# Moving small work between engines and queues in a fused attention and expert kernel

## The chip, the cores and the metric

The kernel runs on one core of a Trainium2 chip. The core has five engines with instruction streams of their own: TensorE (PE, matrix products; its weight loads are shown apart as PEld), VectorE (DVE), ScalarE (ACT), GpSimd (POOL) and SyncE (SP), which here only issues DMA transfers. The metric is the device time of one execution in microseconds. The kernel before took 1471.6 us (median of three runs, 1470.6 to 1475.58).

## The reference

Four batches of 1024 rows with 512 features, in f32:

```python
x = x + xattn(layernorm(x), ctx, ctx)       # 16 heads of 32; query s sees the keys t < s, row 0 sees itself
x = x + ffn(layernorm(x))

# ffn, in groups of t = 32 rows
logits = einsum('bgtd,des->bgtes', grouped, controller) + tie    # 32 x 4 expert sets
perm = (logits == max over t)                                    # each expert set picks one row of a group
dispatched = einsum('bgtd,bgtes->bgesd', grouped, perm)
inner = relu(einsum('bgesd,desf->bgesf', dispatched, f1) + bias)
out = einsum('bgesd,bgtes->bgtd', einsum('bgesf,esfd->bgesd', inner, f2), perm)
```

## The kernel before, in words

**Attention** (`attention_phase`, L38 to L891). A unit `u` is one batch (`u // 4`) and one group of four heads (`u % 4`), so there are 16 units. For each, PE projects queries, keys and values (`pq` L288, `pk` L274, `pv` L307), then goes through 12 steps: two halves `h` of 512 queries, with 4 and 8 blocks of 128 keys. The scores are computed twice: with queries in the partitions (`sc`, L401 and L407) for the row maxima that VectorE takes (`nm`, L413), and transposed with the maxima subtracted (`st`, L467 and L473). ScalarE makes the exponentials `pr` from the second (L481), and GpSimd clears what the mask forbids (L484).

A step's `pr` then has two uses. PE multiplies it with the values, `av` (L517, in `weigh_values`), two steps later. And its sum over the keys, for the division of the softmax, is gathered elementwise in an accumulator: `add_sums` (L490 to L506), once for each of two groups `g` of two heads. Group 0 is added on VectorE, one step late; group 1 on GpSimd.

At the end of a half, ScalarE copies `av` to `raw` (L526), a single buffer; so the multiply that reads the earlier `raw` is finished first. `normalize` (L531) lets PE sum the accumulators (`pd`, L543), VectorE invert (`rd`, L550), and sends the inverse through DRAM to spread it over partitions: one store (L553) and four loads (L556). The multiply by it (L538) gives `atT`. The last half of all spreads the inverse with PE instead (`pb`, L577).

**Beside it.** For the next batch, `ln_rows` (L198) loads x in two halves (`xt`) and takes the row statistics on VectorE (L211, L212), then a power on GpSimd (L215) and a store of the statistics (L216). `ln_turned` (L227) loads x transposed and the statistics, spread over partitions (`both`, L235). For the batch before, `o_step` (L339) makes the output projection of a row tile (`po`, L348), adds the residual (L354), stores the sum to `x2_dram` (L355) and takes its statistics for the second layernorm (L336, L337). `load_residual` (L324) loads x of a row tile one tile ahead (L327) and adds the bias `bo_sb` on GpSimd (L328); three buffers.

**What sets the order.** A planner in the program's text does. Pieces of VectorE work are put aside with an estimated cost by `later`; `beside(0.9)` takes some from the queue at every step, and `finish(names)` does named ones at once. Matmul work waits in other queues and fills the time in which scores aren't free. PE, VectorE, ScalarE and GpSimd then execute in the order of the text (`manual_schedule`, L1123). SyncE isn't listed there: the framework places its DMAs when the program is built. Each engine executes its own stream in order, and SyncE waits in order as well.

**Routing** (L775 to L891). After the last unit the 4096 rows are taken in eight parts `q` of four row tiles. `load_tokens` loads a part of `x2_dram` (1 MB, L796); `roots` (L817) adds epsilon to variances on VectorE (L819) and raises each part to the power -0.5 on GpSimd (L822); `normalize_tokens` (L824) normalises and stores the part; `turn_tokens` transposes it on PE (`px`, L839); `choose_tokens` makes the logits (`pl`, L845) and the choice; `return_choice` transposes and stores that. The last batch's eight row tiles are projected in between by `last_row` (L800, `po` L808).

**Experts** (`ffn_phase`). The normalised rows are loaded again (`xn`, L939, eight pieces of 1 MB: a quarter of the features and half of the rows), and the choices (`perm`, L1004, in two halves); PE dispatches (`pd`, L957) and makes the first layer (`pi`, L976), then the second layer, and combines.

Of the kernel before, what the change touches and what calls it, by code (L numbers as in the profile page):

```python
# [11 lines left out]
F32 = mybir.dt.float32  # L12
# [25 lines left out]
def attention_phase(  # L38
# [159 lines left out]
    def ln_rows(b):  # L198

        stats = {}  # L200

        def load(half):
            xt = qpool.tile([P, 4, D], F32, tag="xt", name=f"xt_{b}_{half}", bufs=1)
            nc.sync.dma_start(xt, x_t[b, half])
            mv = spool.tile([P, 2, 4], F32, tag="ln_both", name=f"ln_both_{b}_{half}")
            stats[half] = (xt, mv)

        def measure(half, i):
            xt, mv = stats[half]
            st = spool.tile([P, 6], F32, tag="ln_stats", name=f"ln_stats_{b}_{half}_{i}")  # L210
            nc.vector.bn_stats(st, xt[:, i, :])  # L211
            nc.vector.bn_aggr(mv[:, :, i], st)  # L212
            if i == 3:
                nc.vector.tensor_scalar_add(mv[:, 1], mv[:, 1], EPS)
                nc.gpsimd.tensor_tensor(mv[:, 1], mv[:, 1], mhalf, ALU.pow)  # L215
                nc.sync.dma_start(  # L216
                    stats_dram[2 * b + half].rearrange("s (i p) -> p s i", p=P), mv
                )
                if half == 0:
                    load(1)  # L220

        load(0)
        for half in range(2):
            for i in range(4):
                later(("m", b, half, i), 1.0, lambda half=half, i=i: measure(half, i))

    def ln_turned(b):  # L227

        both = {}
        xnTs[b] = qpool.tile([P, NC, S], F32, tag="xnT", name=f"xnT_{b}", bufs=1)  # L230
        nc.sync.dma_start(xnTs[b], xT[b].rearrange("(c p) t -> p c t", p=P))

        def spread_stats(half):
            both[half] = qpool.tile([P, 2, HS], F32, tag="both", name=f"both_{b}_{half}", bufs=1)
            nc.sync.dma_start(both[half], stats_dram[2 * b + half].partition_broadcast(P))  # L235

        def normalize_chunk(half, c):
            xn = xnTs[b][:, c, ts(half, HS)]
            nc.vector.tensor_tensor(xn, xn, both[half][:, 0], ALU.subtract)
            nc.vector.tensor_tensor(xn, xn, both[half][:, 1], ALU.mult)  # L240
            if half == 0 and c == NC - 1:
                spread_stats(1)

        finish(*(("m", b, half, i) for half in range(2) for i in range(4)))
        spread_stats(0)
        for half in range(2):
            later(("wait", b, half), 0.9, lambda: None)
            for c in range(NC):
                later(("n", b, half, c), 1.3, lambda half=half, c=c: normalize_chunk(half, c))
# [74 lines left out]
    def load_residual(b, t):  # L324
        finish(("row", b, t - 3), ("row", b - 1, t + 5))
        xt = opool.tile([P, D], F32, tag="xr", name=f"xr_{b}_{t}", bufs=3)
        nc.sync.dma_start(xt, x[b, ts(t, P), :])  # L327
        nc.gpsimd.tensor_tensor(xt, xt, bo_sb, ALU.add)  # L328
        residuals[b, t] = xt


    moments = opool.tile([P, B * NT, 2], F32, tag="moments", name="moments")

    def measure_row(b, t, x2):
        st = opool.tile([P, 6], F32, tag="row_stats", name=f"row_stats_{b}_{t}", bufs=2)
# [3 lines left out]
    def o_step(b, t, ahead=None):  # L339

        if (b, t) not in residuals:
            load_residual(b, t)
        if ahead:
            load_residual(*ahead)
        finish(*(("at", b * NC + c, t // 4) for c in range(NC)))
        po = ps_m.tile([P, D], F32, tag="pm", name=f"po_{b}_{t}")
        for c in range(NC):
            nc.tensor.matmul(  # L348
                po, lhsT=atTs[b * NC + c][:, ts(t, P)], rhs=weights["o"][:, c, :],
                start=(c == 0), stop=(c == NC - 1),  # L350
            )
            yield (LARGE,) if c < NC - 1 else (LARGE, dve, 0.7)
        xt = residuals.pop((b, t))
        nc.vector.tensor_tensor(xt, po, xt, ALU.add)  # L354
        nc.sync.dma_start(x2_dram[ds(b * S + t * P, P), :], xt)  # L355
        later(("row", b, t), 0.9, lambda: measure_row(b, t, xt), front=True)
# [151 lines left out]
    def weigh_values(u, k):  # L508
# [12 lines left out]
        now[0] += LARGE * (HS - q0) / HS + 0.14  # L521
        if j == last:
            given(act, 0.6)
            finish(("at", u - 1 + h, 1 - h))
            raw = qpool.tile([P, HS], F32, tag="raw", name=f"raw_{u}_{h}", bufs=1)
            nc.scalar.copy(raw, avs.pop((u, h)))  # L526
            avs[u, h] = raw
        if k:
# [2 lines left out]
    def normalize(u, h):  # L531
# [18 lines left out]
        nc.vector.reciprocal(rd, pd)  # L550
        if (u, h) != (NU - 1, 1):
            n = 2 * u + h
            nc.sync.dma_start(inverse_dram[ts(n, P), :], rd)  # L553
            rows = qpool.tile([P, 4, P], F32, tag="inverse", name=f"inverse_{u}_{h}", bufs=1)
            for r in range(R):
# [136 lines left out]
    for u in range(-1, NU):  # L692
# [15 lines left out]
        if more and hc == 1:  # L708
            load_ctx(b + 1, 0)
            add("t", b + 1, [ln_step_turned(b + 1)], 0.0)  # L710
        add("v", u + 1, v_todo)
        if more and hc == 2:
            add("c", b + 1, [load_step(b + 1, 1)], 0.0)
# [7 lines left out]
        for k in range(STEPS):  # L721
# [24 lines left out]
            if u >= 0:  # L746
# [10 lines left out]
                            ensure(("o", u // NC - 1, NT - 1))  # L757
                        soon.append((now[0], normalize(u, h)))

                add_sums(u, k, 1, nc.gpsimd)  # L760
                sums.append(add_first)
                pending.append(weigh)
            slot(2 * (STEPS - k) - 1, scores_free() if u + 1 < NU else 0.0)
    while sums:
# [10 lines left out]
    ES, T = P, 32  # L775
    QN = 4
    NQ = B * S // (QN * P)
    rpool = ctx.enter_context(tc.tile_pool(name="route", bufs=2, reuse_waits="tile"))
    lpool = ctx.enter_context(tc.tile_pool(name="route_last", bufs=2, reuse_waits="tile"))
    xpool = ctx.enter_context(tc.tile_pool(name="route_x", bufs=2, reuse_waits="tile"))  # L780
    ps_o = ctx.enter_context(tc.tile_pool(name="ps_ro", bufs=2, space=PSUM, reuse_waits="tile"))
    ps_x = ctx.enter_context(tc.tile_pool(name="ps_rx", bufs=3, space=PSUM, reuse_waits="tile"))
    ps_l = ctx.enter_context(tc.tile_pool(name="ps_rl", bufs=2, space=PSUM, reuse_waits="tile"))
# [2 lines left out]
    nc.sync.dma_start(ctrl_sb, ctrl.rearrange("(c p) e -> p c e", p=P))  # L786
    tie_sb = rpool.tile([P, T], F32, tag="tie", name="tie_sb", bufs=1)
    nc.sync.dma_start(tie_sb, tie)
    rstd = opool.tile([P, B * NT], F32, tag="rstd", name="rstd")
    tokens, turned, chosen = {}, {}, {}  # L790
    LAST = NQ - NT // QN

# [7 lines left out]
    def last_row(t):  # L800
# [2 lines left out]
            tokens[q] = lpool.tile([P, QN, D], F32, tag="x2l", name=f"x2_{q}")  # L803
        if t + 1 < NT:
            load_residual(B - 1, t + 1)
        po = ps_o.tile([P, D], F32, tag="po", name=f"po_{B - 1}_{t}")
        for c in range(NC):
            nc.tensor.matmul(  # L808
# [1 line left out]
                start=(c == 0), stop=(c == NC - 1),  # L810
            )
        x2 = tokens[q][:, i, :]
        nc.vector.tensor_tensor(x2, po, residuals.pop((B - 1, t)), ALU.add)
        nc.sync.dma_start(x2_dram[ds((B - 1) * S + t * P, P), :], x2)
        measure_row(B - 1, t, x2)

    def roots(q0, q1):  # L817
        r = rstd[:, q0 * QN : q1 * QN]
        nc.vector.tensor_scalar_add(r, moments[:, q0 * QN : q1 * QN, 1], EPS)  # L819
        for q in range(q0, q1):  # L820
            rq = rstd[:, ts(q, QN)]
            nc.gpsimd.tensor_tensor(rq, rq, mhalf, ALU.pow)  # L822

    def normalize_tokens(q):  # L824
        for i in range(QN):
# [45 lines left out]
    load_tokens(0)  # L871
    load_tokens(1)
    load_residual(B - 1, 0)
    roots(0, LAST)
    normalize_tokens(0)
    for n in range(NQ + 2):
        for i in range(QN):
            if n < NQ:
# [9 lines left out]
        for t in range(2 * n, min(2 * n + 2, NT)):  # L888
            last_row(t)
        if 2 * n + 2 == NT:  # L890
            roots(LAST, NQ)  # L891


@with_exitstack
# [272 lines left out]
```

## Time and profile before

| | |
|---|---|
| median of three runs | 1471.6 us |
| profiled execution | 1467.71 us |
| its span | 1465.9 us |
| PE busy | 1393.4 us (95%) |
| VectorE busy | 927.5 us (63%) |
| ScalarE busy | 502.4 us (34%) |
| GpSimd busy | 486.6 us (33%) |
| DMA moved | 125.25 MB, mean 85 GB/s |

The profile is of one execution. Attention takes the span up to about 1144 us, routing up to about 1229, and the experts the rest. Rows of instructions give start, duration, engine, line, tile written and tiles read, and in brackets the idle time of the engine ahead of it with what ended that. Rows of stretches give each engine's busy time, then the clock that TensorE was granted (1.00 is full speed), the busy share of the DMA engines and what they moved. Rows of waits give the total, the number and the longest.

### The profile page before, as it was taken

The page shows a single profiled execution, that of the slowest core. Times are in us where ns is not written, and L with a number is a line of the kernel's source. Part 1 is how long each engine was busy: PE and PEld are TensorE (multiplying, and loading weights), DVE is VectorE, ACT ScalarE, POOL GpSimd, SP SyncE. Part 2 cuts the span into 40 slices and gives each one's busy share as a digit, 9 for nine tenths or more (in the row PEclk, how much of TensorE's full clock was granted, in tenths as well). Part 3 has the DMA queues.
Part 4 walks back from the last instruction along what each step waited for, and adds up shares of the span by engine and source line. Part 5 has one row for each costly group of instructions (what it writes and reads, how often), then busy time and mean ns, then how long its engine had stood idle before and what let it go on. Part 6 is the DMA issues. An engine that isn't in the chain of part 4 may idle for free.

```text
span 1465.9 us, 31695 instructions
## 1 busy us (share of the span) xinstructions
PE 1393.4 (95%) x13704; PEld 733.0 (50%) x13704; DVE 927.5 (63%) x1377; ACT 502.4 (34%) x785; POOL 486.6 (33%) x557
## 2 busy tenths in 40 slices
PE   6999999999899999999999999999998898997997
PEld 4344544445344533543535344434443555887887
DVE  3666777656558586666666766565674464576666
ACT  2033333323132223332322232323334123645664
POOL 1034344333425253434343434333356320000122
PEclk9999999999999999999999999999999797899999
DMA  8011202001230210011212000010112679657554
GB/s 298 26 48 35 77 24 67 20 1 41 57 105 30 89 53 10 11 56 40 86 44 62 30 19 11 10 38 10 39 39 76 222 245 327 178 164 235 184 165 146
DMA packets 96972, 125.25 MB, mean 85 GB/s; under 512 B 12992, under 2 KB 54336, under 8 KB 96704
## 3 DMA queue, kind: packets, MB, share of 16 engines
q1 hardware_dynamic: 94272, 114.84, 25.0%
q0 software_dynamic: 2560, 8.39, 1.9%
q8 instruction: 107, 1.75, 0.5%
q14 instruction: 33, 0.27, 0.1%
HBM read 91.78 MB, written 31.42 MB: 84 GB/s over the span
## 4 chain that ended last, share of the span: by engine, by line
PE 80%; issue 6%; DVE 6%; DMA 3%; POOL 2%; ACT 1%; SPq 0%; POOLq 0%; DVEq 0%; ACTq 0%
PE sc L401 12%; PE st L467 10%; PE av L517 9%; PE pq L288 8%; PE pk L274 8%; PE pv L307 8%; PE po L348 5%; PE pd L957 3%; PE sc L407 3%; DVE nm L413 2%; PE pi L976 2%; PE st L473 2%; PE po L808 2%; PE pl L845 2%; PE pd L543 2%
## 5 line engine op out<-in xcount | busy, mean ns | idle before, releaser
L413 DVE TENSOR_REDUCE nm<-sc 128x2 f32<-128x1024 f32 (+3 forms) x384 | 349.2, 951 | 264.3 <-PE sc L407 179.1
L481 ACT ACTIVATE pr<-st 128x1024 f32<-128x1024 f32 (+3 forms) x384 | 290.4, 808 | 584.3 <-PE st L473 563.1
L484 POOL TENSOR_SCALAR_AFFINE_SELECT pr<-pr 128x256 f32<-128x256 f32 x256 | 122.2, 487 | 383.5 <-ACT pr L481 381.4
L504 POOL TENSOR_TENSOR acc<-acc,pr 128x1024 f32<-128x1024 f32 (+3 forms) x128 | 209.4, 1636 | 93.3 <-ACT pr L481 85.6
L401 PE MATMUL sc<-kT,qT 32*128 32x512 f32 (+3 forms) x1536 | 206.3, 531 | 8.6 <-ACT pr L481 4.9
L467 PE MATMUL st<-qT,kT 32*128 32x512 f32 (+3 forms) x1536 | 191.1, 534 | 4.7 <-DVE nm L413 4.6
L517 PE MATMUL av<-pr,v 128*32 128x512 f32 (+3 forms) x1536 | 166.4, 501 | 7.8 <-POOL pr L484 4.3
L274 PE MATMUL pk<-ct,w_k 128*128 128x512 f32 x256 | 131.0, 629 | 9.9 <-DMA w_k<-in_wkT_dram 9.2
L307 PEld LDWEIGHTS pv<-w_v,ct 128*128 128x128 f32 x1024 | 119.5, 192 | 34.6 <-issue 24.7
L467 PEld LDWEIGHTS st<-qT,kT 32*128 32x128 f32 x1536 | 68.6, 183 | 127.6 <-issue 99.9
L401 PEld LDWEIGHTS sc<-kT,qT 32*128 32x128 f32 x1536 | 74.4, 183 | 115.4 <-issue 50.6
L504 DVE TENSOR_TENSOR acc<-acc,pr 128x1024 f32<-128x1024 f32 (+3 forms) x128 | 126.2, 986 | 9.2 <-POOL pr L484 8.9
L307 PE MATMUL pv<-w_v,ct 128*128 128x128 f32 x1024 | 131.4, 281 | 0.2 <-DMA w_v<-in_wvT_dram 0.2
L288 PE MATMUL pq<-xnT,w_q 128*128 128x512 f32 x256 | 127.3, 616 | 1.5 <-ACT xnT L194 1.5
L501 POOL TENSOR_TENSOR acc<-pr,pr 128x768 f32<-128x768 f32 (+1 forms) x32 | 66.7, 2085 | 161.5 <-ACT pr L481 161.5
L1078 POOL DMA_DIRECT2D out_dram<-xr x32 | 24.2, 757 | 238.8 <-DVE xr L1077 237.6
L348 PE MATMUL po<-w_o,atT 128*128 128x512 f32 x192 | 95.5, 616 | 0.0
L517 PEld LDWEIGHTS av<-pr,v 128*32 128x32 f32 x1536 | 32.0, 108 | 95.0 <-issue 67.2
L274 PEld LDWEIGHTS pk<-ct,w_k 128*128 128x128 f32 x256 | 43.9, 194 | 68.9 <-issue 55.0
L473 PE MATMUL st<-mxT,ones 32*128 32x512 bf16 (+3 forms) x768 | 74.6, 322 | 0.3 <-DVE mxT L444 0.3
L288 PEld LDWEIGHTS pq<-xnT,w_q 128*128 128x128 f32 x256 | 43.0, 189 | 52.9 <-issue 46.2
L967 DVE COPY disp<-pd 128x512 f32<-128x512 f32 x64 | 41.2, 686 | 33.0 <-PE pd L957 30.1
(101 smaller groups left out, 1499.7 us busy)
## 6 DMA issues: line engine op xcount, KB each, us to landing
ct<-in_ctxT_dram SPq DMA_DIRECT2D x8, 1024.0 KB, 5.1
xt<-in_x_dram SPq DMA_DIRECT2D x8, 1024.0 KB, 5.4
xr<-in_x_dram SPq DMA_DIRECT2D x32, 256.0 KB, 2.7
xn_dram<-x SPq DMA_DIRECT2D x8, 1024.0 KB, 5.7
xn<-xn_dram SPq DMA_DIRECT2D x8, 1024.0 KB, 5.5
f<-in_f_dram SPq DMA_DIRECT2D x16, 512.0 KB, 4.5
f<-in_f_dram SPq DMA_DIRECT2D x32, 256.0 KB, 5.9
xr<-x_dram SPq DMA_DIRECT2D x32, 256.0 KB, 4.7
```

The lines of the kernel that those rows point to most:

```text
L274: nc.tensor.matmul(pk, lhsT=weights["k"][:, c, ts(hc, P)], rhs=cts[b, half][:, c, :], start=(c == 0), stop=(c == NC - 1),)
L288: nc.tensor.matmul(pq, lhsT=weights["q"][:, c, ts(hc, P)], rhs=xnTs[b][:, c, ts(half, HS)], start=(c == 0), stop=(c == NC - 1),)
L307: nc.tensor.matmul(pv[:, t, :], lhsT=cts[b, half][:, c, ts(t, P)], rhs=weights["v"][:, c, ts(hc, P)], start=(c == 0), stop=(c == NC - 1),)
L348: nc.tensor.matmul(po, lhsT=atTs[b * NC + c][:, ts(t, P)], rhs=weights["o"][:, c, :], start=(c == 0), stop=(c == NC - 1),)
L401: nc.tensor.matmul(scs[r // 2][:, r % 2, :n], lhsT=qT[rr, ts(i, P)], rhs=kT[rr, ds(c0, n)], start=True, stop=not diag,)
L413: nc.vector.tensor_reduce(nm[:, c0 // HS, i % 4, ts(g, 2)], scs[g][:, :, :n], AX.X, ALU.max, negate=True)
L467: nc.tensor.matmul(scs[r // 2][:, r % 2, :n], lhsT=kT[rr, ts(j, P)], rhs=qT[rr, ds(h * HS + q0, n)], start=True, stop=False,)
L473: nc.tensor.matmul(scs[r // 2][:, r % 2, :n], lhsT=ones16[rr, :], rhs=mxT[rr, ds(q0, n)], start=False, stop=True,)
L481: nc.scalar.activation(pr[:, :, :n], scs[g][:, :, :n], AF.Exp)
L484: nc.gpsimd.affine_select(out=d, in_=d, compare_op=ALU.is_ge, fill=0.0, base=0 if j == 0 else -1, pattern=[[0, 2], [P + 1, P]], channel_mu ...
L504: engine.tensor_tensor(acc, acc, pr[:, :, :n], ALU.add)
L517: nc.tensor.matmul(avs[u, h][rr, q0:], lhsT=vs[u][:, j, rr], rhs=pr[r // 2][:, r % 2, : HS - q0], start=(j == 0), stop=(j == last),)
```

## The change

The changed kernel computes the same. It does the following.

1. `ln_rows`: two empty pieces of 0.9 go ahead of each half's statistics, and one behind; the power, the store of the statistics and the load of the second half become a piece of their own behind it. `ln_turned` finishes that piece too.
2. `load_residual` only loads; the bias is added by `residual`, called at the start of `o_step` and of `last_row`.
3. The epsilons and powers of the second layernorm: those of batches 0 and 1 are taken within attention, at the first unit of batches 2 and 3, behind the rows' statistics; at the start of routing only batch 2's remain, issued behind part 0's normalisation. Batch 3's stay where they were.
4. The `raw` of the last unit's first half takes the buffer of `both`, so the multiply isn't finished ahead of it; in `normalize` the multiply is now finished ahead of the store of the inverse.
5. In the last unit both groups of sums are added on VectorE, one step late.
6. Routing's pools are opened in another order, so its tiles lie elsewhere in SBUF.

The order of SyncE's DMAs follows from the build and changes with this. Ahead of batch 2's `both` load now stand the `inverse` loads of the unit's half before. In routing, `ctrl_sb` and `tie_sb` stand ahead of part 0's load, which waits for the last `pd`. At the dispatch, the first half of `perm` stands ahead of the first `xn` load.

```diff
@@ ln_rows
             if i == 3:
                 nc.vector.tensor_scalar_add(mv[:, 1], mv[:, 1], EPS)
-                nc.gpsimd.tensor_tensor(mv[:, 1], mv[:, 1], mhalf, ALU.pow)
-                nc.sync.dma_start(
-                    stats_dram[2 * b + half].rearrange("s (i p) -> p s i", p=P), mv
-                )
-                if half == 0:
-                    load(1)
+
+        def root(half):
+            mv = stats[half][1]
+            nc.gpsimd.tensor_tensor(mv[:, 1], mv[:, 1], mhalf, ALU.pow)
+            nc.sync.dma_start(stats_dram[2 * b + half].rearrange("s (i p) -> p s i", p=P), mv)
+            if half == 0:
+                load(1)
 
         load(0)
         for half in range(2):
+            for i in range(2):
+                later(("load", b, half, i), 0.9, lambda: None)
             for i in range(4):
                 later(("m", b, half, i), 1.0, lambda half=half, i=i: measure(half, i))
+            later(("behind", b, half), 0.9, lambda: None)
+            later(("m", b, half, 4), 0.0, lambda half=half: root(half))
@@ ln_turned
-        finish(*(("m", b, half, i) for half in range(2) for i in range(4)))
+        finish(*(("m", b, half, i) for half in range(2) for i in range(5)))
@@ load_residual
         nc.sync.dma_start(xt, x[b, ts(t, P), :])
+        residuals[b, t] = xt
+
+    def residual(b, t):
+        xt = residuals.pop((b, t))
         nc.gpsimd.tensor_tensor(xt, xt, bo_sb, ALU.add)
-        residuals[b, t] = xt
+        return xt
...
+    rstd = opool.tile([P, B * NT], F32, tag="rstd", name="rstd")
+
+    def variances(t0, t1):
+        nc.vector.tensor_scalar_add(rstd[:, t0:t1], moments[:, t0:t1, 1], EPS)
+
+    def roots(t0, t1):
+
+        for t in range(t0, t1, 4):
+            rt = rstd[:, ds(t, 4)]
+            nc.gpsimd.tensor_tensor(rt, rt, mhalf, ALU.pow)
@@ o_step
+        xt = residual(b, t)
         finish(*(("at", b * NC + c, t // 4) for c in range(NC)))
...
-        xt = residuals.pop((b, t))
@@ weigh_values
-            finish(("at", u - 1 + h, 1 - h))
-            raw = qpool.tile([P, HS], F32, tag="raw", name=f"raw_{u}_{h}", bufs=1)
+            if (u, h) == (NU - 1, 0):
+
+                raw = qpool.tile([P, 2, HS], F32, tag="both", name=f"raw_{u}_{h}", bufs=1)[:, 0]
+            else:
+                finish(("at", u - 1 + h, 1 - h))
+                raw = qpool.tile([P, HS], F32, tag="raw", name=f"raw_{u}_{h}", bufs=1)
@@ normalize
             n = 2 * u + h
+            finish(("at", u - 1 + h, 1 - h))
             nc.sync.dma_start(inverse_dram[ts(n, P), :], rd)
@@ the loop over units
+        if b > 1 and hc == 0:
+            finish(*(("row", b - 2, t) for t in range(NT)))
+            t0 = (b - 2) * NT
+            later(("variances", b), 0.3, lambda t0=t0: variances(t0, t0 + NT))
+            for half in range(2):
+                later(("behind roots", b, half), 0.9, lambda: None)
+                later(("roots", b, half), 0.0, lambda t=t0 + 4 * half: roots(t, t + 4))
...
-                add_sums(u, k, 1, nc.gpsimd)
-                sums.append(add_first)
+                if u < NU - 1:
+                    add_sums(u, k, 1, nc.gpsimd)
+                    sums.append(add_first)
+                else:
+                    sums.append(lambda u=u, k=k: (add_first(u, k), add_sums(u, k, 1, nc.vector)))
@@ routing
+    xpool = ctx.enter_context(tc.tile_pool(name="route_x", bufs=2, reuse_waits="tile"))
     rpool = ctx.enter_context(tc.tile_pool(name="route", bufs=2, reuse_waits="tile"))
     lpool = ctx.enter_context(tc.tile_pool(name="route_last", bufs=2, reuse_waits="tile"))
-    xpool = ctx.enter_context(tc.tile_pool(name="route_x", bufs=2, reuse_waits="tile"))
...
-    rstd = opool.tile([P, B * NT], F32, tag="rstd", name="rstd")
@@ last_row
+        xt = residual(B - 1, t)
...
-        nc.vector.tensor_tensor(x2, po, residuals.pop((B - 1, t)), ALU.add)
+        nc.vector.tensor_tensor(x2, po, xt, ALU.add)
...
-    def roots(q0, q1):
-        r = rstd[:, q0 * QN : q1 * QN]
-        nc.vector.tensor_scalar_add(r, moments[:, q0 * QN : q1 * QN, 1], EPS)
-        for q in range(q0, q1):
-            rq = rstd[:, ts(q, QN)]
-            nc.gpsimd.tensor_tensor(rq, rq, mhalf, ALU.pow)
...
-    roots(0, LAST)
     normalize_tokens(0)
+    variances((B - 2) * NT, (B - 1) * NT)
+    roots((B - 2) * NT, (B - 1) * NT)
...
-            roots(LAST, NQ)
+            variances((B - 1) * NT, B * NT)
+            roots((B - 1) * NT, B * NT)
```

## The prediction

> **What bounds the kernel now.** I read the page's busy shares first, then PE's waits, then the instructions around the two longest ones that the edits touch.
>
> ```profile
> PE 1393.4 (95%) x13704; PEld 733.0 (50%) x13704; DVE 927.5 (63%) x1377; ACT 502.4 (34%) x785; POOL 486.6 (33%) x557
> ...
> PE st L467 <- DVE nm L413: 4.6, 1, 4.6
> PE av L517 <- POOL pr L484: 4.3, 3, 1.8
> ...
> PE av L517 <- ACT raw L526: 3.4, 5, 2.6
> ```
>
> TensorE (PE) is busy 1393.4 of 1465.9 us and the change leaves its matmuls alone. So a gain can only come out of its 72.5 us of idle time, and out of stretches in which its clock is granted at half. The three waits (us in total, times, longest) are those that this diff can reach; together they hold 12.3 us. The largest wait of all, 9.2 us for w_k at the start, is not touched.
>
> The first wait is one event, at 375 us. SyncE's own issues, then VectorE and PE:
>
> ```profile
> 356.11 0.38 SPq L216 DMA_DIRECT2D stats_dram<-ln_both  x1
> 356.79 0.34 SPq L553 DMA_DIRECT2D inverse_dram<-rd  x1
> 367.49 0.34 SPq L235 DMA_DIRECT2D both<-stats_dram  x1
> 368.15 1.71 SPq L556 DMA_DIRECT2D inverse<-inverse_dram  x4
> ...
> 372.74 0.69 DVE L538 TENSOR_TENSOR atT<-raw,inverse 128x512 f32<-128x512 f32 x1 [7.91 <-DMA inverse<-inverse_dram]
> ...
> 375.42 1.22 PE L467 MATMUL st<-qT,kT 32*128 32x512 f32 x2 [4.62 <-DVE nm L413]
> ```
>
> The `both` load must wait until the statistics store has landed, 11.4 us after it was issued. The four `inverse` loads stand behind it in SyncE's queue, though their own store had little to wait for (elsewhere the same pair is 1.6 us apart: 1122.51 and 1124.11). The multiply into atT is 7.91 us late, the maxima behind it on VectorE are late, and PE stands.
>
> The other two waits are the last unit (`raw` 2.63, the masks on GpSimd 1.83, 1.51 and 0.96). Stretches of 15 us (PE, PEld, DVE, ACT, POOL busy; granted clock; DMA share; GB/s):
>
> ```profile
> 360.00:375.00 15.00, 10.79 (x84) 5.62 (x82) 6.37 (x9) 3.19 (x4) 4.70 (x2) 0.96 0.18 54
> 375.00:390.00 15.00, 14.59 (x63) 5.05 (x63) 7.75 (x11) 4.04 (x5) 5.68 (x6) 0.81 0.00 0
> ...
> 1110.00:1125.00 15.00, 12.37 (x100) 4.94 (x102) 6.40 (x8) 6.29 (x7) 4.82 (x3) 0.89 0.27 80
> 1125.00:1140.00 15.00, 10.71 (x116) 4.42 (x110) 4.72 (x6) 5.78 (x9) 14.32 (x14) 0.83 0.27 88
> 1140.00:1155.00 15.00, 11.15 (x46) 7.70 (x39) 6.22 (x16) 2.34 (x4) 9.05 (x9) 0.60 0.69 229
> ...
> 1230.00:1245.00 15.00, 12.34 (x160) 10.87 (x158) 6.01 (x10) 5.39 (x11) 0.00 (x0) 0.52 1.07 337
> ```
>
> At 1125 us GpSimd is busy 14.32 of 15 and sets the pace; VectorE has 10 us free.
>
> **1. SyncE's order, and the statistics' placement.** In the built order of the changed program the `inverse` loads of that unit follow their store directly, ahead of batch 2's statistics. So the 4.21 us that PE lacks at 360 to 375 come back, and of the half clock after it 15 x 0.19 = 2.85 us. The clock gate is where a rule can be set against the row. The Trainium skill ("TensorE: Matmul & The Clock Gate", Part 1) says that the clock falls to half after a window of some 3.4 us of idleness and returns after as long a busy one. The row agrees for this wait of 4.62. But by the rule the last unit's gaps (2.63, 1.83, 1.51) would cost only their own length, 6.9 us with the 0.96; the rows there show 0.89 and 0.83 as well, 15 x (0.11 + 0.17) = 4.2 us more. I go by the rows. Term A: -7.0. What may be late next: the `both` load's wait of about 11 us doesn't vanish; it now stands, near 393 to 404 us, in front of an x2 store and the next residual load. VectorE's four row statistics of the second half come in one block of 4 x (0.68 + 0.18) + 0.3 = 3.7 us. Both stand at places where PE had no wait. If that cover fails for one of the three batches, it is another event like this one, so A's range is -8 to 0.
>
> **2. Small work on GpSimd.** The residual's bias add (1.27 us each) moves from the row's load to its use; its waits for that load, 38.2 us in six, go from in front of GpSimd's masks. PE waits for GpSimd only in the last unit, so this is nothing now. Cover: VectorE needs the sum only after the row's four po matmuls, 1.85 us (half of 3.70 for eight), which is longer than 1.27; behind a big GpSimd sum (2.35) the add may come up to 2 us late for VectorE, which is 63% busy. If a residual load is late, the add still waits in GpSimd's queue with masks and sums behind it, and PE's av behind those; with the load one row ahead I see no such case. Four of the six powers (about 1.03 each) and two adds of 0.17 go into attention where GpSimd is a third busy: nothing. Sum: 0, range 0 to +2.
>
> **3. The last unit.** Eleven copies and sums move from GpSimd to VectorE. PE alone, from 1115.2 without its waits and at full clock: av, pd, st and the rest are 14.0 us of work by the rows at full clock (1.06 for an av of 512, 1.06 for a pd, 1.3 for an st), so 1129.3. VectorE from 1112 on: eight sums of 128x1024 at 1.22 = 9.8; two each of 1.14 and 0.87 and 0.60 make 5.2; xr 0.68, its statistics 0.87, rd 0.96 and two atT at 0.69: 18.9 us in all. With about 1 us of waits for exponentials it ends near 1132, and pd after it near 1133.2. Before, pd ended at 1140.74. Term L: -7.5. VectorE becomes this unit's bound. A GpSimd sum beside a VectorE one seems to slow the latter (1.43 against 1.16), so I keep 1.22. If VectorE is also late for the first exponentials, or the atT wait (landing 5.4 us after rd) holds the sums behind it, -4; if it overlaps better, -10.
>
> **4. The junction.** Before, px at 1146.63 waits 2.62 for the normalised x2_0, which had waited for the adds and the first power:
>
> ```profile
> 1140.78 0.96 DVE L550 RECIPROCAL rd<-pd 128x128 f32<-128x128 f32 x1 [2.18 <-PE pd L543]
> ...
> 1144.98 6.17 POOL L822 TENSOR_TENSOR rstd<-rstd,mhalf 128x4 f32<-128x4 f32 x6 [4.55 <-DVE rstd L819]
> ...
> 1146.63 3.68 PE L839 MATMUL px<-ident,x 128*128 128x128 f32 x16 [2.62 <-DVE x L827]
> ```
>
> That is 5.9 us after pd. The power goes from this path. But the routing pools open in another order, and the built program now gives x2_0's load (before at 1125.87, long landed) a wait for the last pd. Such a 1 MB load lands in 5.5 us (median of six), and x2_1's is right behind and shares the queues: 5.5 + 0.6 for the hand-over and a share of the second + 0.55 to normalise = about 6.7. So one wait takes the place of the other: +0.8, range -1 to +3. The clock of 0.60 at 1140 stays low, since px still waits: 0.
>
> **5. Routing to dispatch.** SyncE's order changes here too. xn_0_0 (1 MB) was read at 1207.84, while the engines still had room. It now stands behind perm h0 and a later write, at about 1225, in a stretch where DMA is at 1.02 to 1.07 of its share. The first dispatch matmuls (1229.54) need it: 1225 + 5.5 to 6.5 is 1231 to 1232. Term D: +2.5, range 0 to +7 (the upper end if all four loads queue and the half clock of 0.52 lasts longer).
>
> Sum: -7.0 + 0 - 7.5 + 0.8 + 2.5 = -11.2. The profiled execution took 1467.71 (1465.9 span and 1.8 around it): 1456.5. The median shown is 3.9 above the profiled one: 1460.4, said as 1460.
>
> **Rivals.**
> - *The wait only moves* (A = 0, perhaps +1: one such wait elsewhere). The `both` load's 11 us stand elsewhere on the same queue, and the residual loads behind them feed GpSimd. For it: the landing took as long in the other batches (11.6 at 642.60). Against: those cost PE nothing. Then 1467.
> - *VectorE fills up* (L = -3). For it: 18.9 us of work in some 20, in strict order with atT's DMA wait between. Then 1465.
> - *Slower.* One mechanism: the `both` load's 11 us wait, now ahead of the x2 stores and residual loads on SyncE in batches 1, 2 and 3, makes residuals late. GpSimd's bias add then waits with the masks behind it, PE stands for av, and the clock falls. Each such event is priced like the one at 375 us: 4.62 + 2.85 = 7.5. One gives back A; two (15.0 against 11.2) bring the time 4 above before, and three give 1467.71 - 11.2 + 22.5 = 1479.0, a median of 1483. From two events on it decides. For it: GpSimd has waited up to 10.4 us for a residual before. Against: those waits cost PE nothing, and a row's load has a whole row's time.
> - *It doesn't do what it says*: the order on SyncE changes, but the multiply at 375 and the last unit are held by something the trace hides (the exponentials, for instance): 1471.
>
> **How the numbers follow.** Forecast 0.60, own range 1453 to 1467; wait moves 0.12; VectorE fills 0.10; slower 0.10; nothing 0.08. About 0.3% (4.4 us) is what a measurement can tell from no change. Faster: 0.57 + 0.06 + 0.07 = 0.70; same: 0.03 + 0.05 + 0.02 + 0.07 = 0.17; slower: 0.01 + 0.01 + 0.10 + 0.01 = 0.13. The range from 1452 to 1474 leaves out the slower case and the best end. It takes in A and L at their small ends and D at its upper one.
>
> **What would show it.** A: no wait of st for nm above 1 us near 375, and a clock of 1.00 at 375 to 390. L: VectorE busy above 12 in the last 15 us before the last pd, the waits for masks gone, pd's end near 1133 less A's 7. Junction: px waits for a DMA of x2_0 rather than a power. D: the first pd of the dispatch with a DMA wait of 2 to 3. Wrong would be: a new PE wait for nm or masks in batches 1 to 3, or px later than 8 us after pd.

## The result and the profile after

The changed kernel takes 1482.45 us (median of 11 runs, 1474.95 to 1487.23) where the kernel before took 1473.22 beside it (11 runs). The ratio is 1.0059, with a 95% interval of 1.0036 to 1.0083: it is slower by about 9 us, where 1460 had been forecast.

The busy shares on the page of the changed kernel, and PE's waits (us in total, times, longest):

```profile
PE 1406.8 (95%) x13704; PEld 734.7 (49%) x13704; DVE 926.8 (62%) x1390; ACT 502.6 (34%) x785; POOL 474.2 (32%) x546
```

```profile
PE px L866 <- DVE x L854: 6.6, 3, 3.7
PE st L486 <- DVE nm L432: 5.8, 3, 2.7
PE pq L293 <- DVE xnT L245: 5.3, 3, 3.7
...
PE pd L986 <- DMA perm<-perm_dram: 2.6, 1, 2.6
...
PE av L536 <- POOL pr L503: 1.6, 4, 0.5
...
PE pd L986 <- DMA xn<-xn_dram: 1.3, 1, 1.3
```

The waits that the prediction aimed at have shrunk: av for GpSimd from 4.3 to 1.6, and av for `raw` is no longer among the waits. But st for nm grew from one event of 4.6 to three with 5.8, and pq now waits 5.3 us for normalised rows (`xnT`), which it didn't before. The stretches (PE, PEld, DVE, ACT, POOL busy; clock; DMA share; GB/s) show both sides:

```profile
195.00:210.00 15.00, 11.66 (x60) 4.57 (x56) 10.84 (x16) 2.33 (x5) 5.05 (x6) 0.77 0.00 0
...
360.00:375.00 15.00, 15.00 (x155) 8.22 (x153) 9.62 (x19) 5.08 (x7) 3.09 (x3) 1.00 0.02 6
375.00:390.00 15.00, 15.00 (x112) 7.62 (x110) 11.26 (x15) 5.81 (x6) 6.24 (x5) 1.00 0.08 25
...
1140.00:1155.00 15.00, 13.59 (x152) 4.67 (x144) 14.55 (x17) 8.66 (x12) 7.19 (x8) 1.00 0.27 75
```

At 360 to 390 PE is busy throughout at full clock, and in the last unit VectorE is busy 14.55 of 15 while PE goes on at 13.59. At 195 there is a new hole.

Where the time went is seen by following one instruction through both traces. The table takes the start of some row maxima (there are 384, in the same order in both), of routing's first logits add and of the last transposed copy, and gives how much later it is after than before. Both spans are of one execution.

| start in the trace before, us | later after by | added since the row above | what lies there |
|---|---|---|---|
| 103.5 | 6.5 | +6.5 | half clock twice between 62 and 83 us |
| 235.0 | 15.2 | +8.7 | batch 1's statistics: the hole at 195 (6.4 of it from 152 on) |
| 418.0 | 7.5 | -7.7 | the wait at 375 is gone |
| 614.1 | 16.2 | +8.7 | batch 2: st at 463, pq and others at 508 to 523 |
| 830.8 | 23.8 | +7.6 | batch 3: pq at 795 |
| 1093.0 | 24.6 | +0.8 | |
| 1162.5 | 16.2 | -8.4 | last unit and junction |
| 1451.0 | 18.6 | +2.4 | dispatch |

The first row isn't the change's: PE's instructions and gaps are the same there in both. The clock was half twice for 6.8 us, also in traces of kernels without part 1 (`last_only`, `before_runs` and `pools_only` below), and not in that of part 1 alone. So the two profiled executions differ by 18.7 us, but the timed runs by about 9.

### The profile page after: what moved, and what is told of

Read it like the earlier page. It is cut to its first block, busy times and chain, and to the rows that moved or that the text cites. A ratio compares the mean times of both kernels' runs of the same rounds, so it can differ in the third digit from the quotient of the medians.

```text
span 1484.6 us, 31733 instructions
## 1 busy us (share of the span) xinstructions
PE 1406.8 (95%) x13704; PEld 734.7 (49%) x13704; DVE 926.8 (62%) x1390; ACT 502.6 (34%) x785; POOL 474.2 (32%) x546
## 3 DMA queue, kind: packets, MB, share of 16 engines
q1 hardware_dynamic: 94272, 114.84, 24.6%
## 4 chain that ended last, share of the span: by engine, by line
PE 79%; DVE 7%; issue 6%; DMA 4%; POOL 2%; ACT 1%; SPq 0%; POOLq 0%; DVEq 0%; ACTq 0%
PE sc L420 12%; PE st L486 10%; PE pk L279 9%; PE pq L293 8%; PE av L536 8%; PE pv L312 7%; PE po L368 5%; DVE nm L432 3%; PE pd L986 3%; PE sc L426 3%; PE pi L1005 2%; PE st L492 2%; DMA inverse_dram<-rd 2%; PE po L842 2%; PE pl L872 2%
## 5 line engine op out<-in xcount | busy, mean ns | idle before, releaser
L503 POOL TENSOR_SCALAR_AFFINE_SELECT pr<-pr 128x256 f32<-128x256 f32 x256 | 128.2, 510 | 427.2 <-ACT pr L500 425.6
L523 POOL TENSOR_TENSOR acc<-acc,pr 128x512 f32<-128x512 f32 (+1 forms) x120 | 194.2, 1618 | 81.0 <-ACT pr L500 71.7
L420 PE MATMUL sc<-kT,qT 32*128 32x512 f32 (+3 forms) x1536 | 210.4, 537 | 8.5 <-ACT pr L500 4.1
L486 PE MATMUL st<-qT,kT 32*128 32x512 f32 (+3 forms) x1536 | 194.1, 536 | 6.1 <-DVE nm L432 5.8
L279 PE MATMUL pk<-ct,w_k 128*128 128x512 f32 x256 | 136.1, 650 | 10.1 <-DMA w_k<-in_wkT_dram 9.3
L293 PE MATMUL pq<-xnT,w_q 128*128 128x512 f32 x256 | 131.2, 631 | 6.7 <-DVE xnT L245 5.3
L523 DVE TENSOR_TENSOR acc<-acc,pr 128x1024 f32<-128x1024 f32 (+3 forms) x136 | 130.6, 967 | 0.3 <-POOL pr L503 0.3
L520 POOL TENSOR_TENSOR acc<-pr,pr 128x768 f32<-128x768 f32 (+1 forms) x30 | 62.6, 2086 | 163.7 <-ACT pr L500 163.7
L996 DVE COPY disp<-pd 128x512 f32<-128x512 f32 x64 | 41.2, 686 | 35.3 <-PE pd L986 32.4
```

Of the source, the lines that this page charges most:

```text
L279: nc.tensor.matmul(pk, lhsT=weights["k"][:, c, ts(hc, P)], rhs=cts[b, half][:, c, :], start=(c == 0), stop=(c == NC - 1),)
L293: nc.tensor.matmul(pq, lhsT=weights["q"][:, c, ts(hc, P)], rhs=xnTs[b][:, c, ts(half, HS)], start=(c == 0), stop=(c == NC - 1),)
L420: nc.tensor.matmul(scs[r // 2][:, r % 2, :n], lhsT=qT[rr, ts(i, P)], rhs=kT[rr, ds(c0, n)], start=True, stop=not diag,)
L486: nc.tensor.matmul(scs[r // 2][:, r % 2, :n], lhsT=kT[rr, ts(j, P)], rhs=qT[rr, ds(h * HS + q0, n)], start=True, stop=False,)
L503: nc.gpsimd.affine_select(out=d, in_=d, compare_op=ALU.is_ge, fill=0.0, base=0 if j == 0 else -1, pattern=[[0, 2], [P + 1, P]], channel_mu ...
L523: engine.tensor_tensor(acc, acc, pr[:, :, :n], ALU.add)
```

## The experiments

Ratios are to the kernel before, run beside each on the same chip, with 95% intervals; they are worked out from the single runs and not from the medians. The changed kernel's 1.0059 and the kernels below were measured in several groups. "The gap" below is the time from the issue of an inverse store to the issue of the loads that wait for it.

**Part 1 undone** (the lines that matter).

```diff
             if i == 3:
                 nc.vector.tensor_scalar_add(mv[:, 1], mv[:, 1], EPS)
-
-        def root(half):
-            mv = stats[half][1]
-            nc.gpsimd.tensor_tensor(mv[:, 1], mv[:, 1], mhalf, ALU.pow)
+                nc.gpsimd.tensor_tensor(mv[:, 1], mv[:, 1], mhalf, ALU.pow)
...
-            for i in range(2):
-                later(("load", b, half, i), 0.9, lambda: None)
...
-            later(("behind", b, half), 0.9, lambda: None)
-            later(("m", b, half, 4), 0.0, lambda half=half: root(half))
```

> The changed kernel with part 1 undone: the statistics of a batch's rows, their power and their store are placed as in the kernel before; parts 2 to 6 stay. Theory (placement): part 1 costs, net, the three stretches of batches 1 to 3 (9 + 9 + 7.5 us in the two profiles) less the 8.3 that it gains at 375 us, about 17 us, so this takes about 1465 us, 8 below before. Rival (small work): the residual's add and the powers that moved on GpSimd are what delays batches 1 to 3; then this still takes about 1482.

Measured: 1477.41 us, ratio 1.0013 (0.9989 to 1.0038). That is better than the changed kernel's 1.0059, but the 1465 of the placement theory isn't reached. The wait at 375 was back (inverse store at 359.30, loads at 371.72), and batch 3 lost 7.2 us between 614 and 781 although its statistics stood where they had been: six of its eight normalising instructions of one half came at one step, 136 (counted in pairs of row maxima), where the kernel before had them at 128 to 131. The rest of the change puts empty pieces into the same queue, ahead of the second layernorm's powers.

**Part 1 alone on the kernel before**, the same edit the other way.

> The kernel before with part 1 alone. Theory (placement): batches 1 to 3 lose about 17 us net, so about 1490 us, with the inverse loads again more than 10 us behind their store where a store of statistics was issued just ahead. Rival (small work): about 1473, like before, or less.

Measured: 1485.14 us, ratio 1.0074 (1.0045 to 1.0104). The placement alone makes the kernel slower; the rival falls. The inverse loads came 11.0 and 11.3 us after their stores at 173 and 438 us, each a store of the inverse just behind one of statistics.

**The statistics store in runs of 32 bytes.** Each partition's eight numbers go out as one piece. The order in memory is wrong for the load, so this kernel's normalisation uses wrong statistics; only its time is of use.

```diff
-            nc.sync.dma_start(stats_dram[2 * b + half].rearrange("s (i p) -> p s i", p=P), mv)
+            nc.sync.dma_start(stats_dram[2 * b + half].rearrange("s (p i) -> (s p i)", p=P).rearrange("(p n) -> p n", p=P), mv.rearrange("p s i -> p (s i)"))
```

> The changed kernel, but the statistics store writes each partition's eight numbers as one run of 32 bytes (128 pieces for 1024 of four bytes), which is the wrong order for the load, so the result is not the reference's; all else and all orders the same. Theory (collision): the 1024 small writes keep the queue of SyncE busy for some 10 us, and an inverse store issued just behind lands late; with 128 pieces the gap from inverse store to load falls from 10.6 and 11.4 to under 4 us, the waits of st for nm in batches 1 and 2 go (2.7 + 2.3, and about 5 us at half clock), so about 1474 us. Rival (lateness): it is the later statistics that make the normalised rows late for the next batch's queries; then the waits of pq for xnT stay and the time stays near 1480.

Measured: 1469.48 us, ratio 0.9976 (0.9954 to 0.9997), 0.0083 below the changed kernel or some 12 us, and more than expected. SyncE's issues of the changed kernel around batch 1's second store:

```profile
179.50 0.38 SPq L219 DMA_DIRECT2D stats_dram<-ln_both  x1
179.97 0.53 SPq L577 DMA_DIRECT2D inverse_dram<-rd  x1
190.53 3.20 SPq L580 DMA_DIRECT2D inverse<-inverse_dram  x4
```

and of this kernel, the same three:

```profile
179.01 0.34 SPq L219 DMA_DIRECT2D stats_dram<-ln_both  x1
179.44 0.38 SPq L577 DMA_DIRECT2D inverse_dram<-rd  x1
181.10 1.71 SPq L580 DMA_DIRECT2D inverse<-inverse_dram  x4
```

Between the store of the inverse and its loads nothing else is issued in either, and no `both` load stands ahead. The loads wait for their own store, which takes 10.6 us to land behind 1024 writes of four bytes and 1.7 behind 128 of 32. In the second event, at 442 us, a 1 MB load of x is issued between the two stores; it is there in this kernel too, with a gap of 1.8 for 11.4. So the order of issue on SyncE, which the prediction blamed at 375 us, isn't needed to make an inverse late: a store of statistics just ahead of the inverse store is enough. The trace before had it as well. Its chain of work gives the inverse store's own way to landing (start, duration):

```profile
356.79 11.34 DMA inverse_dram<-rd
```

That ends at 368.13, and the loads were issued at 368.15. The DMA engines weren't full meanwhile: from 360 to 367 us of that trace their busy share is 0.01 and 2 GB/s move, and from 182 to 190 us of the changed kernel's it is 0.02 and 1.

In the changed kernel VectorE stands 6.94 us for the second such event, and PE 2.31; first VectorE's row, then PE's:

```profile
461.35 0.69 DVE L561 TENSOR_TENSOR atT<-raw,inverse 128x512 f32<-128x512 f32 x1 [6.94 <-DMA inverse<-inverse_dram]
```

```profile
463.23 0.70 PE L486 MATMUL st<-qT,kT 32*128 32x512 f32 x2 [2.31 <-DVE nm L432]
```

The 5.3 us of pq for xnT stayed, as the lateness theory had it: both theories hold a part. Set against the trace before, as in the table, this kernel loses 0.3 us from 152 to 235 where the changed one loses 6.4, and 4.2 from 418 to 614 for 8.7, but 7.3 from 614 to 831 for 7.6. So the collisions make about 11 us of the traces, and batch 3's loss isn't theirs.

**The store issued by GpSimd.**

```diff
-            nc.sync.dma_start(stats_dram[2 * b + half].rearrange("s (i p) -> p s i", p=P), mv)
+            nc.gpsimd.dma_start(stats_dram[2 * b + half].rearrange("s (i p) -> p s i", p=P), mv)
```

> The changed kernel, but the statistics store is issued by GpSimd, behind the power that it waits for. Theory (collision): SyncE's queue is free of the small writes, so the inverse round trip is under 4 us again, and the time about 1474 us, if issuing 1024 pieces costs GpSimd less than 3 us each of six times. If it's the engines of the DMA that are shared and not the queue, the inverse stays late and the time near 1482.

Measured: 1475.18 us, ratio 1.0006 (0.9979 to 1.0032). Batch 1's long gap went, but those at 444 and 731 us were still 8.7 and 7.9 (11.4 and 7.0 in the changed kernel). Another issuer brings back 0.0053 of the ratio, where longer pieces brought 0.0083, and leaves two of three long gaps.

**The last unit alone** (parts 4 and 5 on the kernel before, `last_only`; part 5's lines).

```diff
-                add_sums(u, k, 1, nc.gpsimd)
-                sums.append(add_first)
+                if u < NU - 1:
+                    add_sums(u, k, 1, nc.gpsimd)
+                    sums.append(add_first)
+                else:
+                    sums.append(lambda u=u, k=k: (add_first(u, k), add_sums(u, k, 1, nc.vector)))
```

> The kernel before with parts 4 and 5 alone (both groups of the last unit's sums on VectorE, its first raw in another buffer). Theory: the four waits of the last unit and the half clock around them go, 8 us as in the profile of the changed kernel, so a ratio to before of about 0.995. Rival (VectorE fills up): VectorE sets the end of the unit, the last pd comes at most 3 us earlier, and the ratio is 0.998 or more.

Measured: 1472.79 us, ratio 0.9973 (0.9958 to 0.9988), about 4 us. In its trace the last unit gave 8.1 us between the row maximum at 1093 and routing's logits, as expected, while the wait at 375 was longer (st for nm 6.3) than in the trace before. The timed gain is between the two theories' numbers; the trace supports the first for the last unit. The gap at that wait was 12.9 us there for 11.4 before; why stays open.

**The kernel before with its statistics in runs** (`before_runs`): the store as above, and the order put right by a strided read in SBUF, whose lines follow.

```diff
-            xn = xnTs[b][:, c, ts(half, HS)]
-            nc.vector.tensor_tensor(xn, xn, both[half][:, 0], ALU.subtract)
-            nc.vector.tensor_tensor(xn, xn, both[half][:, 1], ALU.mult)
+            xn = xnTs[b][:, c, ts(half, HS)].rearrange("q (i p) -> q i p", p=P)
+            rows = both[half].rearrange("q a h -> q (a h)").rearrange("q (p s i) -> q s i p", s=2, i=4)
+            nc.vector.tensor_tensor(xn, xn, rows[:, 0], ALU.subtract)
+            nc.vector.tensor_tensor(xn, xn, rows[:, 1], ALU.mult)
```

> The kernel before, whose statistics store writes each partition's eight numbers as one run of 32 bytes, while the normalisation reads them from SBUF with that stride, so that the result is the same; nothing else. Theory (collision): the one wait at 375 us and its half clock come from the inverse store standing behind 1024 small writes; gap from inverse store to load under 4 us there, wait of st for nm gone, 7 to 8 us less, ratio about 0.995. Rival (order on SyncE, as the prediction had it): the inverse loads still stand behind the load of the statistics, which still waits for its store; if that landing stays near 11 us the wait stays, ratio 1.00. A strided read that costs VectorE more than 0.1 us on each of 48 would show in its rows.

Measured: 1474.3 us, ratio 0.9978 (0.9961 to 0.9996). The gap at 370 us fell from 11.4 to 4.1 us with the order on SyncE unchanged. The gain is less than half of the expected one, and the strided read isn't cheap. The medians rise from 683 and 773 ns in the kernel before to (min/median/max):

```profile
L238 DVE TENSOR_TENSOR xnT<-xnT,both x24: 1070/1085/1302, 183.6 to 844.6; 128x512 f32<-128x512 f32 x24
L239 DVE TENSOR_TENSOR xnT<-xnT,both x24: 1092/1182/3274, 184.7 to 845.9; 128x512 f32<-128x512 f32 x24
```

In its trace 5.1 us more than before passed between 152 and 235. There one of batch 1's multiplies took 3.27 us on VectorE (at 241.92), the maxima behind it were late, and PE stood for 3.11.

**The two kernels before this in one** (the last unit and the runs).

> The kernel before with parts 4 and 5 and with the statistics stored in runs of 32 bytes; the result is the same. Theory: both gains add up, ratio about 0.990 (15 us less than before). If they collide somewhere, between 0.990 and 0.995.

Measured: 1468.45 us, ratio 0.9938 (0.9919 to 0.9958). The gains add up to about what the two single kernels showed (0.0027 + 0.0022 = 0.0049, measured 0.0062), not to 0.010; the end between 0.990 and 0.995 holds. The strided read's cost had been left out; the same 5.0 us are lost by 235.

**The changed kernel with the pools as before** (part 6 undone, three lines).

```diff
-    xpool = ctx.enter_context(tc.tile_pool(name="route_x", bufs=2, reuse_waits="tile"))
     rpool = ctx.enter_context(tc.tile_pool(name="route", bufs=2, reuse_waits="tile"))
     lpool = ctx.enter_context(tc.tile_pool(name="route_last", bufs=2, reuse_waits="tile"))
+    xpool = ctx.enter_context(tc.tile_pool(name="route_x", bufs=2, reuse_waits="tile"))
```

> The changed kernel with the routing pools in the order before. Theory: the part's first load no longer waits for the last pd, and the first xn load of the dispatch stands ahead of perm again: px about 1 us sooner after the last pd and the first layer 2.5 us sooner, so 2 to 4 us less than the changed kernel (ratio to before about 1.003). Rival: the late loads are hidden, same as the changed kernel (1.006).

Measured: 1479.56 us, ratio 1.0008 (0.9993 to 1.0023), 0.005 below the changed kernel. In its trace px waited 1.5 us at most where the changed kernel has 3.7, and the half clock at the junction was gone.

**Part 6 alone on the kernel before** (`pools_only`).

> The kernel before with part 6 alone: part 0's load waits for the last pd, and the first xn load comes behind perm. Theory: 5 us at the junction (px waits for the load, and a longer half clock) and 2 to 4 at the dispatch, a ratio of 1.005. Rival (the prediction's own sizes): 0.8 + 2.5, ratio 1.002.

Measured: 1471.54 us, ratio 1.000 (0.998 to 1.002). Both numbers expected are too high: the 1.005 is excluded, the 1.002 sits at the interval's end. Before, px waits for the power anyway, some 6 us after the last pd, and the load that starts there takes as long. In this trace px comes 6.3 us after the last pd, for 5.9. The load comes to count only where part 3 has taken the power away: with it gone and the pools as before, px came after 3.7. At the dispatch this trace has 5.2 us more than before, which the timed runs don't bear out.

**The changed kernel with runs and the pools as before** (`runs_pools`; store, strided read and pools as above).

> The changed kernel with the statistics stored in runs of 32 bytes (read with that stride, the result is the same) and the routing pools in the order before; parts 1 to 5 stay. Theory: both repairs add up, 0.0083 and 0.0051 of the ratio (store in runs 0.9976, pools 1.0008, against 1.0059), so 0.992 to 0.994. If either was another chip's luck, above 0.997.

Measured: 1480.81 us, ratio 1.0049 (1.0027 to 1.0072). The expectation was wrong by 0.012. It had left out the strided read. All gaps are under 4 us here, and PE waits longer than in the changed kernel:

```profile
PE pq L294 <- DVE xnT L246: 7.8, 4, 4.4
PE st L487 <- DVE nm L433: 7.1, 3, 3.1
```

What was left, the normalisation in blocks, grew as each pair of its instructions did (2.27 us for 1.38). That fits the theory that the blocks are what costs, which the next kernel puts to the test.

**The same without the empty pieces.**

```diff
-            for i in range(2):
-                later(("load", b, half, i), 0.9, lambda: None)
...
-            later(("behind", b, half), 0.9, lambda: None)
...
-                later(("behind roots", b, half), 0.9, lambda: None)
```

> As runs_pools, but without the empty pieces of 0.9 ahead of and behind the statistics and ahead of the powers, so that the normalisation of batches 2 and 3 is spread over single steps again and not done in blocks of four and eight ahead of the next batch's query projection. Theory (block): the waits of pq for xnT (5.3 us, longest 3.7) go with the half clock behind them; in the profile batch 2 lost 5.1 and batch 3 6.6 us that the stored runs did not give back, so 8 to 11 us less than runs_pools, a ratio of 0.985 to 0.988. Rival: the blocks are hidden, and the time is that of runs_pools.

Measured: 1458.76 us, ratio 0.9907 (0.9876 to 0.9937), 0.0142 below runs_pools, with the same dear reads. The waits of pq for xnT are gone from its list, and of the difference to runs_pools in the traces 9.7 us lie between 418 and 614 and 12.6 between 614 and 831. The block theory holds: spread over steps, the same instructions are hidden there. (Not everywhere: the 5.0 us between 152 and 235 are lost here too.) Its size had been expected at half (8 to 11 us of difference; 0.0142 is 21).

**The changed kernel without the empty pieces alone**, all else as changed.

> The changed kernel without the empty pieces of 0.9 alone (two ahead of each half's statistics, one behind, one ahead of each pair of powers); the store in small writes and the pools stay as changed. Theory: the statistics fall on the steps they had before, so the blocks of normalisation go, and of the collisions only one is left, as before; against no_blanks (0.991) it keeps the pools' order (0.005) and one collision (0.003 to 0.005), so a ratio of 0.998 to 1.001. Rival: the empty pieces are not what made batches 1 to 3 slower, and it stays at 1.005 or more.

Measured: 1461.67 us (1456.81 to 1465.43), ratio 0.9929 (0.9901 to 0.9956), where 0.998 to 1.001 was expected. The power and the store, a piece of their own now, fall behind the inverse's round trip instead of ahead of it:

```profile
366.84 0.34 SPq L574 DMA_DIRECT2D inverse_dram<-rd  x1
370.14 1.70 SPq L577 DMA_DIRECT2D inverse<-inverse_dram  x4
375.78 0.38 SPq L219 DMA_DIRECT2D stats_dram<-ln_both  x1
```

Not one collision is left (the longest gap is 4.8 us), and st waits for nm 2.0 us in all (three times, 0.9 at most). The empty pieces thus cost 0.0130 of the ratio, some 19 us, and turn a change that would gain some 10 us (0.0071) into one that loses 9.

## Why the prediction was wrong

**The first part's term A, and its cover.** The step that failed is "Both stand at places where PE had no wait", with A's range of -8 to 0. The wait at 375 went as forecast (-7.7 by the table for -7.0), but each of the three batches got a loss of its own, 8.7, 8.7 and 7.6: A was about +17 us in the traces. The sign of being wrong that the prediction had named, a new wait of PE for nm in batches 1 to 3, is there at 198.6 (2.65 us) and 463.2 (2.31). The forecast looked for what the moved statistics put on SyncE and VectorE at their new place, and only for the `both` load and the block of statistics. Two things were missed. By the program's text each comes of the slots in the planner's queue: three empty pieces and four statistics make seven for a half and 14 for a batch, where there were eight, and a unit has 12 steps. The last experiment bears that out, as it takes away nothing but empty pieces.

First, the stores themselves moved. A store of statistics just ahead of an inverse store stretches the gap from about 1.6 to some 11 us, whatever the order of loads. The kernel before met that once (356 us). The changed kernel has it at 179.50, at 442.08 and, with a gap of 7.0, at 733.83. The prediction had the right rows in hand (store, store, 0.7 us apart) and read the wrong cause from them: the `both` load between, which only shares the wait. That the inverse's own store "had little to wait for" was a misreading; it took 11.34 us to land. With the right one, each of six stores had to be held against the next inverse store.

Second, normalisation begins late. Its pieces wait in the planner's queue, and the next batch's first query projection finishes what is left at once. Before, they came in four steps for batch 3's first half (128 to 131, a pair at each); after, all eight instructions stand at step 136 (four of them with part 1 alone, six with parts 2 to 6 alone). The first two pairs before, with row maxima between them:

```profile
729.59 0.68 DVE L239 TENSOR_TENSOR xnT<-xnT,both 128x512 f32<-128x512 f32 x1
730.30 2.72 DVE L240 TENSOR_TENSOR xnT<-xnT,both 128x512 f32<-128x512 f32 x1
732.94 2.34 DVE L413 TENSOR_REDUCE nm<-sc 128x2 f32<-128x1024 f32 x2
...
736.94 0.89 DVE L239 TENSOR_TENSOR xnT<-xnT,both 128x512 f32<-128x512 f32 x1
737.86 0.77 DVE L240 TENSOR_TENSOR xnT<-xnT,both 128x512 f32<-128x512 f32 x1
```

After, PE's rows at the projection, and the start of VectorE's block that it waits for:

```profile
791.46 0.40 PE L426 MATMUL sc<-mask_strict,ident 128*128 128x128 bf16 x4
795.52 3.78 PE L293 MATMUL pq<-xnT,w_q 128*128 128x512 f32 x4 [3.66 <-DVE xnT L245]
```

```profile
791.79 2.36 DVE L432 TENSOR_REDUCE nm<-sc 128x2 f32<-128x1024 f32 x2 [1.06 <-PE sc L426]
794.06 0.68 DVE L244 TENSOR_TENSOR xnT<-xnT,both 128x512 f32<-128x512 f32 x1
794.78 0.69 DVE L245 TENSOR_TENSOR xnT<-xnT,both 128x512 f32<-128x512 f32 x1
795.38 0.69 DVE L244 TENSOR_TENSOR xnT<-xnT,both 128x512 f32<-128x512 f32 x1
```

PE stands for the maxima and the first pair, and its clock is half for 6.8 us from 792.85 on (0.84 at 795 to 810). The trace before couldn't show this wait; the order of the changed program could, by counting how many normalising instructions stand together ahead of each pq.

**The slower rival** had the right sign and size for an event (7.5 us; the table gives 8.7, 8.7 and 7.6 for the three batches) and the wrong mechanism, so it is luck that its 1483 for three events comes so close to the measured 1482.45. No residual load held GpSimd's masks: outside the last unit PE doesn't wait for them. The residual's move cost nothing that shows, as forecast in part 2, though no kernel undoes it alone. Part 3's empty pieces helped to make batch 3's block.

**The last unit** was right in the trace. From the row maximum at 1093.0 to the end of the last pd it took 47.7 us before (1140.7) and 39.2 after (1117.6 to 1156.8): 8.5, for -7.5. VectorE became the bound as forecast, with eight sums in a row at the end, 7.21 us in all. Timed alone, parts 4 and 5 brought about 4 us (2 to 6 by the interval), so the full 7.5 isn't shown there.

**The junction** was about right. px starts 6.0 us after the last pd (1156.8 to 1162.88), for 5.9 before and 6.7 forecast; it waits for a DMA of x2_0, as said. That the clock stays low held too (half for 6.8 us from 1161.5).

**The dispatch** was right: +2.4 from routing's first logits to the end, for +2.5, with PE waiting 1.3 for xn and 2.6 for perm.

As a sum the forecast is borne out by the last experiment: without the empty pieces the ratio is 0.9929, and 1460 against 1471.6 is 0.992. That says nothing of single terms, and there the wait at 375 goes for another reason than the forecast's: the store of statistics falls behind the inverse's round trip.

## What to carry to other kernels

When a store of many small pieces is moved, look at every transfer that is issued in the 10 us behind it, not only at the loads that wait for it. When work is put into a planner's queue with padding, count slots against the deadline at which the rest is forced: a few empty ones can turn hidden single instructions into a block ahead of the busiest engine. And where two waits end together, taking one away shows the other; the pools' order cost nothing until the power was gone.

## What had not been expected of the hardware

The small writes: where a load waits for them, 1024 of four bytes (4 KB in all) take 8 to 12 us to land in the kernels before and after (store at 694.58, load at 702.82; 642.60 and 654.17), 128 of 32 bytes 1.4 (683.42 and 684.84, in the first kernel with runs) and up to 4.3 in `before_runs`. What is issued just behind waits with them (10.6 us at 180 us, with a DMA share of 0.02). GpSimd as issuer didn't free the others altogether.

A VectorE operand read with a stride of 32 bytes costs some 0.4 us more on a 128x512 f32 instruction (medians from 0.683 to 1.085 and from 0.773 to 1.182). The Trainium skill ("SBUF — State Buffer", Door 1) has a rule that fits: SBUF is read in lines of 16 bytes, and an access that goes to a new line each time pays. Between steps most of it was hidden, but 5 us were lost at one place (152 to 235 us); ahead of a projection the blocks of runs_pools grew with it.

TensorE's clock differs between executions of the same stretch. In the profile of the kernel before it was full from 12 to 374 us. In those of ten of the other thirteen kernels it was half twice for 6.8 us between about 62 and 83 us, with the same PE work and no gap of PE above 0.8 us; the same instructions take 41.2 to 41.5 us there and 35.1 in the other four. In the changed kernel the clock also fell, for 6.8 us from 198.9 and for 3.4 from 465.2, behind waits of 2.65 and 2.31 us. By the rule of the Trainium skill that the prediction weighed ("TensorE: Matmul & The Clock Gate", Part 1: some 3.4 us of idleness) none of these gaps is long enough alone, so what takes the clock there stays open. The profile of before was a favourable one. Over the timed runs of one kernel the time falls by 0.9 to 1.6 us for each 0.001 of mean clock, which is most of their spread: a difference of 9 us between kernels needs many runs, and a trace of each shows a few us of chance.
